# A graph layer on one core: sums kept in PSUM for a block, residual added from PSUM, one buffer for products

## The chip, the cores and the metric

The kernel runs on one core of a Trainium2 chip. The metric is the device time of one execution in microseconds (us). Engines are named as in the profile: PE (TensorE matmuls), PEld (its weight loads), DVE (VectorE), ACT (ScalarE), POOL (GpSimd) and SP (SyncE, which issues most of the transfers). Each engine works through its own queue in order, and semaphores hold an instruction until what it reads is written and what it overwrites is read.

## The reference

There are 6,250 nodes with 64 features and 206,250 edges, sorted by their destination node.

```
h   = relu(layernorm(x))                       # 6250 x 64
msg = h[src] + edge_attr                       # 206250 x 64
agg = segment_sum(msg, dst)                    # 6250 x 64
out = x + relu(agg @ W1 + b1) @ W2 + b2        # 64 -> 128 -> 64
```

## The kernel before

The sum over the edges is split in two. For the features of nodes, `h[src]`, most edges are handled without a gather. A matrix of counts (how often node s feeds node d) is made by matmuls of masks, and then multiplied by h. For the features of edges, matmuls of masks with the edges' own rows give the sums directly.

**Blocks and steps.** The nodes are taken in 23 blocks (`NW`). The first 22 have 14 steps each, and the last has 10. `count(b, s)` at each step makes the counts of six lists of edges. PE runs six products of masks into a PSUM tile `pc` (line 868), and ACT copies the tile to `counts` in SBUF (line 871). There are two `pc` tiles, so the products of step n wait for the copy of step n-2. Every third step DVE makes the masks `hot_lo` and `hot_key` of three steps (line 858), with two buffers each.

**Products.** The counts of block b-1 are multiplied by h during steps 0 to 6 of block b (`multiply`, line 888). They accumulate in a PSUM tile `pv`, of which there are two. At step 3 `chunk_place` (line 461) adds the edges' sums of block b-1 into the same `pv`. At step 10 `add_products` (line 900) lets DVE add `pv` to the sums in SBUF.

**Sums of edges.** A block has up to six chunks of 42 nodes, taken in two at a time. Such a pair is called a set (a unit in the code). At steps 7, 10 and 13 `chunk_sum` runs 24 small matmuls per chunk into one PSUM tile `bank` (line 439). Right behind them ACT copies the set to SBUF as `by_node` (line 442), and SP issues the loads of the set after the next (line 418). `chunk_place` of the next block reads the three copies. In the first block the sums stand at steps 10, 12 and 13, and in the last block at 6 and 8.

**Groups.** The last 20 groups of edges have no counts. POOL gathers rows of h onto their edge features (line 301), and `sum_groups` (line 489) sums two groups at a time, also in `bank`. ACT copies that to `by_group` (line 492). These sums fall on steps 0, 1, 2 or 4 of some blocks.

**Layers.** For a block of nodes whose sum is complete, `mlp` puts five parts on the steps n, n+2, n+9, n+10 and n+11, with n at step 8 or 11. `mlp_hidden` multiplies by W1 (line 936) and ACT applies relu (line 938). `mlp_product` multiplies by W2 into the PSUM tile `po` (line 943), and ACT copies it to `y` (line 949). `bias` adds b2 to the rows of x (line 928). `mlp_add` adds those to `y` on DVE (line 954), and `mlp_store` sends `y` out. At the very end `mlp_out` (line 959) adds from `po` without a copy.

**Order.** The order of each engine's queue is written out by hand. The loop over `steps` at the end of the program emits the work of a step in a fixed order: `before` entries, count, multiply, place, add, layers, then the entries put there by `at(step, ...)`, and last the groups. Where a gather stands is planned with times written into the program (`pool_until`). [...]

The opening, up to about 40 us, normalises x, finds where the lists of edges begin and packs them. There `by_quarters` (line 651) uses `pv` tiles for four small products `psrcq`.

Of the kernel before, what the change touches and what calls it, by code (L numbers as in the profile page):

```python
# [116 lines left out]
AHEAD = 16  # L117
OPENING_US = 15.0
# [3 lines left out]
def gnn_kernel(ctx: ExitStack, tc: tile.TileContext, x, src_t, dst_t, dst_g, edge, w1, b1, w2, b2, out):  # L122
# [277 lines left out]
    bank = ps.tile([P, GB * D], F32, name="bank", bufs=1)  # L400
# [5 lines left out]
    assert sum(n for _, _, n in units) == NC  # L406
    unplaced = [sum(1 for unit in units if unit[0] == b) for b in range(NW)]
# [24 lines left out]
    def chunk_sum(u):  # L432
        n = units[u][2]
        hot, feat = hot_of.pop(u), feats.pop(u)
        for i in range(n):
            for k in range(JP):
                for q in range(JQ):
                    j = q * JP + k
                    nc.tensor.matmul(bank[q * QP:q * QP + WQ, i * D:(i + 1) * D], hot[:, i, j, :], feat[i][:, j, :],  # L439
                                     start=(k == 0), stop=(k == JP - 1))  # L440
        by_node[u] = work.tile([P, GB, D], F32, name="by_node", bufs=3)
        nc.scalar.activation(by_node[u][:, :n].rearrange("p c d -> p (c d)"), bank[:, :n * D], AF.Copy)  # L442
        load(u + 2)

# [9 lines left out]
    def chunk_place(u):  # L454
        b, c, n = units[u]
        of = by_node.pop(u)
# [27 lines left out]
    def sum_groups(g, hot, tiles):  # L484
        for b in range(GB):
            for k in range(PK):
                for q in range(PQ):
                    j = q * PK + k
                    nc.tensor.matmul(bank[q * QP:q * QP + WQ, b * D:(b + 1) * D], hot[:, b, j, :],  # L489
                                     tiles[b][:, j, :], start=(k == 0), stop=(k == PK - 1))  # L490
        by_node["h", g] = work.tile([P, GB, D], F32, name="by_group", bufs=1)
        nc.scalar.activation(by_node["h", g].rearrange("p b d -> p (b d)"), bank, AF.Copy)  # L492
# [152 lines left out]
    def by_quarters(t0, t1):  # L645
        rows = src_s.bitcast(F32)
        for t in range(t0, t1):
            own = slice(t * QP, (t + 1) * QP)
            px = ps.tile([P, 512], F32, tag="pv", name="psrcq")[:, :GP * PK]
# [225 lines left out]
    def open_pv(b):  # L875
        pvs[b] = [ps.tile([P, 512], F32, tag="pv", name="pv")[:, :BN], 0]
# [62 lines left out]

    def mlp_rows(b, tag="po", bufs=1):  # L940
        po = ps.tile([P, 2, D], F32, tag=tag, name="po", bufs=bufs)
# [4 lines left out]
    def mlp_product(b):  # L946
        po = mlp_rows(b)
        y = late.tile([NP, 2, D], F32, name="y", bufs=2)
        nc.scalar.activation(y[:pairs[b]], po[:pairs[b]], AF.Copy)  # L949
        outs[b] = y  # L950

    def mlp_add(b):
        y = outs[b]
        nc.vector.tensor_tensor(y[:pairs[b]], y[:pairs[b]], xs.pop(b)[:pairs[b]], op=OP.add)
# [148 lines left out]
    ADDED, LOADED = 10, 2  # L1103
# [17 lines left out]
    for u, (b, c, _) in enumerate(units):  # L1121
# [4 lines left out]
        at(n, chunk_sum, u)  # L1126

# [211 lines left out]
```

## Time and profile before

| what | value |
|---|---|
| median of 3 runs | 489.25 us (488.44 to 490.86) |
| the profiled execution | 489.07 us, span 487.2 us |
| PE busy | 424.2 us (87%) |
| DVE busy | 415.1 us (85%) |
| POOL busy | 388.3 us (80%) |
| ACT busy | 366.0 us (75%) |

A group's row in the profile reads: line, engine, operation, output <- inputs by the program's names, shapes, count, then busy us, mean ns of one, and the idle time of the engine before them with what ended it. A row of the timeline reads: start in us from the begin of the span, length in us, engine, line, operation, and in brackets the idle time of the engine before it and what ended that. Rows of one kind that follow each other are merged (x12 stands for 12 matmuls). The ends of matmuls are modelled, so a few hundredths of a us between PE and another engine mean little.

### The profile page before, as it was taken

To read this page: it belongs to the slowest core of one execution; us is meant where nothing else is said; L and a number is where in the kernel's file an instruction comes from. 1 tells how busy PE (TensorE), PEld (TensorE's weight loads), DVE (VectorE), ACT (ScalarE), POOL (GpSimd) and SP (SyncE) were. 2 spreads that over 40 slices of the span, in tenths; PEclk is the share of its full clock that TensorE was granted. 3 is DMA by queue.
4 is the path that set the end of the run, shared out by engine and by line. 5 is a ranking of instruction groups with operands and counts; after the bars stand their busy time and mean duration, and the time that the engine had idled before them with its cause. 6 is when DMAs were issued, how large, how long until landed. Compare 5 with 4: busy or idle time off the path is not lost.

```text
span 487.2 us, 17218 instructions
## 1 busy us (share of the span) xinstructions
PE 424.2 (87%) x7301; PEld 374.8 (77%) x7302; DVE 415.1 (85%) x561; ACT 366.0 (75%) x607; POOL 388.3 (80%) x239
## 2 busy tenths in 40 slices
PE   3156798998988999999999999989999999999894
PEld 3055687886886888888988978878888888888783
DVE  7888989879999798988998889888998899998751
ACT  3727889878877788788898789777887787786650
POOL 7787888888888888888888888888888888888000
PEclk9655699999999999999999999999999999999998
DMA  9959367378366585784784784675775775764700
GB/s 237 238 172 300 74 147 193 76 180 192 69 167 155 145 228 122 176 230 105 192 220 98 172 228 94 170 201 125 187 187 124 201 179 122 203 158 93 213 13 16
DMA packets 122378, 77.98 MB, mean 160 GB/s; under 512 B 34768, under 2 KB 120728, under 8 KB 122072
## 3 DMA queue, kind: packets, MB, share of 16 engines
q1 hardware_dynamic: 97464, 66.88, 47.1%
q0 software_dynamic: 24592, 9.19, 15.0%
q8 instruction: 59, 0.97, 0.8%
q10 hardware_dynamic: 240, 0.75, 0.5%
q14 instruction: 23, 0.19, 0.1%
HBM read 72.80 MB, written 3.99 MB: 158 GB/s over the span
## 4 chain that ended last, share of the span: by engine, by line
PE 68%; ACT 13%; DMA 6%; issue 5%; DVE 4%; POOL 3%; DVEq 0%; ACTq 0%; POOLq 0%
PE pv L888 26%; PE pc L868 22%; PE bank L439 11%; ACT counts L871 9%; POOL rows L301 3%; DMA feat<-in_edge 3%; PE po L943 2%; PE pv L461 2%; DMA dstq<-in_dst_g,cols_i 2%; ACT junk L694 1%; PE ph L936 1%; PE bank L489 1%; DVE hot_key L858 1%; DVE hot_lo L858 1%; DMA firsts_i<-in_dst_g 1%
## 5 line engine op out<-in xcount | busy, mean ns | idle before, releaser
L301 POOL DMA_INDIRECT pfeat<-table,src_p x160 | 334.0, 2088 | 49.7 <-issue 43.0
L871 ACT ACTIVATE counts<-pc 128x882 fp32r<-128x882 f32 x318 | 282.1, 916 | 49.1 <-PE pc L868 39.8
L868 PE MATMUL pc<-hot_key,hot_lo 128*128 128x147 bf16 x1908 | 179.2, 232 | 22.9 <-ACT counts L871 13.6
L858 DVE TENSOR_TENSOR hot_lo<-iota_lo,keys 128x2304 bf16<-128x2304 bf16 (+1 forms) x107 | 143.8, 1344 | 36.2 <-PE pc L868 29.0
L888 PE MATMUL pv<-counts,h 128*128 128x252 f32 (+1 forms) x1127 | 171.0, 292 | 0.2
L868 PEld LDWEIGHTS <-hot_lo 128*128 128x128 bf16 x1908 | 130.5, 100 | 45.4 <-issue 24.2
L858 DVE TENSOR_TENSOR hot_key<-iota_key,keys 128x2664 bf16<-128x2664 bf16 (+1 forms) x107 | 163.3, 1526 | 0.0
L888 PEld LDWEIGHTS pv<-counts,h 128*128 128x128 f32 x1127 | 143.5, 190 | 0.6 <-ACT counts L871 0.5
L439 PE MATMUL bank<-feat,hot 128*21 128x64 f32 x3240 | 69.0, 222 | 5.9 <-issue 3.0
L439 PEld LDWEIGHTS bank<-feat,hot 128*21 128x21 f32 x3240 | 52.3, 101 | 18.3 <-issue 6.8
L427 DVE TENSOR_TENSOR hot<-rel,iota 128x504 f32<-128x504 bf16 x68 | 45.6, 671 | 0.1
L442 ACT ACTIVATE by_node<-bank 128x128 f32<-128x128 f32 x68 | 19.0, 280 | 18.4 <-PE bank L439 12.4
L301 POOL DMA_INDIRECT words<-packed,first_i x15 | 20.8, 1385 | 4.6 <-issue 3.4
L301 POOL DMA_INDIRECT rows<-in_dst_g,row_i x15 | 17.4, 1162 | 5.2 <-issue 4.0
L943 PE MATMUL po<-w2s,hid 128*126 128x64 f32 (+2 forms) x100 | 16.8, 288 | 1.7 <-ACT hid L938 1.2
L943 PEld LDWEIGHTS po<-w2s,hid 128*126 128x126 f32 (+2 forms) x100 | 13.5, 192 | 5.7 <-ACT hid L938 1.9
L936 PE MATMUL ph<-sums,w1s 128*128 128x252 f32 (+2 forms) x50 | 16.1, 404 | 0.2 <-ACT y L949 0.2
L900 DVE TENSOR_TENSOR sums<-sums,pv 128x252 f32<-128x252 f32 (+4 forms) x31 | 9.8, 339 | 6.7 <-PE pv L888 5.9
L492 ACT ACTIVATE by_group<-bank 128x128 f32<-128x128 f32 x10 | 2.8, 277 | 15.1 <-PE bank L489 11.1
L938 ACT ACTIVATE hid<-ph,b1s 128x252 f32<-128x252 f32 (+2 forms) x25 | 11.6, 464 | 2.3 <-PE ph L936 2.3
L461 PE MATMUL pv<-select,by_node 128*64 128x42 f32 (+1 forms) x272 | 12.6, 234 | 0.0
L461 PEld LDWEIGHTS pv<-select,by_node 128*64 128x64 f32 x272 | 9.9, 137 | 3.0
(202 smaller groups left out, 252.3 us busy)
## 6 DMA issues: line engine op xcount, KB each, us to landing
feat<-in_edge SPq DMA_DIRECT2D x135, 384.0 KB
pfeat<-in_edge SPq DMA_DIRECT2D x20, 256.0 KB
pfeat<-table,src_p POOLq DMA_INDIRECT x160
xl<-in_x SPq DMA_DIRECT2D x2, 768.0 KB
xs<-in_x SPq DMA_DIRECT2D x23, 63.0 KB
out_y<-y SPq DMA_DIRECT2D x23, 63.0 KB
dstn<-in_dst_g SPq DMA_DIRECT2D x1, 1024.0 KB
table<-xl SPq DMA_DIRECT2D x1, 800.0 KB
```

The costliest lines, as they stand in the source:

```text
L301: nc.gpsimd.indirect_dma_start(out=rows, out_offset=None, in_=source, in_offset=bass.IndirectOffsetOnAxis(ap=index, axis=0), compute_op=op)
L427: nc.vector.tensor_tensor(hot_of[u][:, :n].rearrange("p c j w -> p (c j) w"), rel[:, c:c + n].rearrange("p c q k -> p (c q k)").unsqueeze( ...
L439: nc.tensor.matmul(bank[q * QP:q * QP + WQ, i * D:(i + 1) * D], hot[:, i, j, :], feat[i][:, j, :], start=(k == 0), stop=(k == JP - 1))
L442: nc.scalar.activation(by_node[u][:, :n].rearrange("p c d -> p (c d)"), bank[:, :n * D], AF.Copy)
L461: nc.tensor.matmul(pvs[b][0][i * D:(i + 1) * D, k:k + z - a], of[:, i, :], select[:, a - low:z - low], start=False, stop=False)
L858: nc.vector.tensor_tensor(hot[:, :n].rearrange("p t (m o) -> p t m o", o=2), iota_k.rearrange("p (m o) -> p m o", o=2).unsqueeze(1).to_bro ...
L868: nc.tensor.matmul(pc[:, k, m * K:(m + 1) * K], hot_lo[:, j, :], hot_key[:, j, :K], start=True, stop=True)
L871: nc.scalar.activation(ring[:, (2 * b + half) % 3, :, i * ST * V:(i + 1) * ST * V].rearrange("p h (k m) -> p h k m", k=2), pc[:, :, :ST // ...
L888: nc.tensor.matmul(pv[:, :2 * half].rearrange("p (k n) -> p k n", k=2), h2[:, h, :], of[:, :, h, :half], start=(h == 0), stop=(h == HI - 1))
L936: nc.tensor.matmul(ph[:, :n], w1s, agg[:, start[b]:start[b + 1]], start=True, stop=True)
L938: nc.scalar.activation(outs[b][:, :n], ph[:, :n], AF.Relu, bias=b1s)
L943: nc.tensor.matmul(po[:pairs[b], k, :], outs[b][:, k:2 * pairs[b]:2], w2s, start=True, stop=True)
```

## The change

The PSUM tile `bank` grows from one set to four (a whole 2 KiB bank). Three are for a block's sets and one for groups. `chunk_sum` writes each set to its own place and no longer copies. For a block but the last, one ACT instruction copies all its sets at step 1 of the next block (`chunk_copy`, `COPIED = 1`). In the last block each set is copied alone, right behind its sums, as before. `by_node` becomes one tile for a whole block instead of three for sets.

`mlp_product` writes to one of four places in a PSUM tile of its own, `rows_p`, and ACT no longer copies it. `mlp_add` adds the residual on DVE straight from PSUM into a new `y`.

The bank for `rows_p` comes from `pv`, which has one buffer instead of two.

```diff
+SETS = 3
...
-    bank = ps.tile([P, GB * D], F32, name="bank", bufs=1)
+    bank = ps.tile([P, SETS + 1, GB, D], F32, name="bank", bufs=1)
     nc.vector.memset(bank, 0.0)
...
+    set_of = [sum(1 for v in units[:u] if v[0] == units[u][0]) for u in range(len(units))]
...
     def chunk_sum(u):
...
-                    nc.tensor.matmul(bank[q * QP:q * QP + WQ, i * D:(i + 1) * D], hot[:, i, j, :], feat[i][:, j, :],
+                    nc.tensor.matmul(bank[q * QP:q * QP + WQ, set_of[u], i, :], hot[:, i, j, :], feat[i][:, j, :],
                                      start=(k == 0), stop=(k == JP - 1))
-        by_node[u] = work.tile([P, GB, D], F32, name="by_node", bufs=3)
-        nc.scalar.activation(by_node[u][:, :n].rearrange("p c d -> p (c d)"), bank[:, :n * D], AF.Copy)
         load(u + 2)
+
+    def chunk_copy(b, u0, u1):
+        if b not in by_node:
+            by_node[b] = work.tile([P, SETS, GB, D], F32, name="by_node", bufs=1)
+        k0, k1 = set_of[u0], set_of[u1] + 1
+        nc.scalar.activation(by_node[b][:, k0:k1].rearrange("p k c d -> p (k c d)"),
+                             bank[:, k0:k1].rearrange("p k c d -> p (k c d)"), AF.Copy)
...
     def chunk_place(u):
-        of = by_node.pop(u)
+        of = by_node[b][:, set_of[u]]
...
     def sum_groups(g, hot, tiles):
-                    nc.tensor.matmul(bank[q * QP:q * QP + WQ, b * D:(b + 1) * D], hot[:, b, j, :],
+                    nc.tensor.matmul(bank[q * QP:q * QP + WQ, SETS, b, :], hot[:, b, j, :],
...
-            px = ps.tile([P, 512], F32, tag="pv", name="psrcq")[:, :GP * PK]
+            px = ps.tile([P, 512], F32, tag="pv", name="psrcq", bufs=1)[:, :GP * PK]
...
-        pvs[b] = [ps.tile([P, 512], F32, tag="pv", name="pv")[:, :BN], 0]
+        pvs[b] = [ps.tile([P, 512], F32, tag="pv", name="pv", bufs=1)[:, :BN], 0]
...
+    rows_p = ps.tile([P, 4, 2, D], F32, name="rows_p", bufs=1)
+    turn_p = [0]
+
     def mlp_rows(b, tag="po", bufs=1):
-        po = ps.tile([P, 2, D], F32, tag=tag, name="po", bufs=bufs)
+        if tag == "pr":
+            po = rows_p[:, turn_p[0] % 4]
+            turn_p[0] += 1
+        else:
+            po = ps.tile([P, 2, D], F32, tag=tag, name="po", bufs=bufs)
...
     def mlp_product(b):
-        po = mlp_rows(b)
-        y = late.tile([NP, 2, D], F32, name="y", bufs=2)
-        nc.scalar.activation(y[:pairs[b]], po[:pairs[b]], AF.Copy)
-        outs[b] = y
+        outs[b] = mlp_rows(b, "pr")

     def mlp_add(b):
-        y = outs[b]
-        nc.vector.tensor_tensor(y[:pairs[b]], y[:pairs[b]], xs.pop(b)[:pairs[b]], op=OP.add)
+        po = outs[b]
+        outs[b] = late.tile([NP, 2, D], F32, name="y", bufs=2)
+        nc.vector.tensor_tensor(outs[b][:pairs[b]], po[:pairs[b]], xs.pop(b)[:pairs[b]], op=OP.add)
...
-    ADDED, LOADED = 10, 2
+    ADDED, LOADED, COPIED = 10, 2, 1
...
         at(n - 1, chunk_hot, u)
         at(n, chunk_sum, u)
+        if b == NW - 1:
+            at(n, chunk_copy, b, u, u)
+        elif unplaced[b] == i + 1:
+            at(first_step[b + 1] + COPIED, chunk_copy, b, u - i, u)
```

3 lines of the change are left out of this document (2 added, 1 removed).

## The prediction

> **What bounds the kernel now.** I read the page first, then the busy time of each engine in the steady stretch, the waits of TensorE, ScalarE and VectorE there, the groups of instructions of the lines that the diff touches, and last the timeline of a few blocks. The profiled execution took 489.07 us for a span of 487.2; the median of the runs is 489.25, so the two stand within 0.2 us, and the sum below is made against 489.07.
>
> ```profile
> 60.00:460.00 400.00, 374.09 (x6706) 331.80 (x6695) 357.36 (x446) 321.01 (x520) 340.55 (x168) 1.00 0.66 163
> ```
>
> In this row of the windows view (length, then PE, PEld, DVE, ACT and POOL busy, clock, DMA share), PE is busy 374 of 400 us and ACT 321. The steady stretch can give back at most PE's 26 us of idle time, and only what ends on ACT can answer to this change. The waits in 60 to 470 us:
>
> ```profile
> PE pc L868 <- ACT counts L871: 12.2, 24, 1.0
> PE bank L439 <- issue: 3.0, 9, 0.5
> PE bank L439 <- DMA feat<-in_edge: 2.0, 2, 1.4
> ...
> PE ph L936 <- ACT y L949: 0.2, 1, 0.2
> ```
> ```profile
> ACT counts L871 <- PE pc L868: 38.5, 89, 1.2
> ```
>
> Each row is total us, times, longest. PE waits 12.2 us for ACT to empty a buffer of products (pc), and ACT waits 38.5 us for PE to fill one. PE is the bound with ACT close behind. The change takes copies out of ACT's queue, so the question is how much of the 12.2 us those copies cause.
>
> **The terms.** Groups by line over the span (busy us, mean ns, idle before):
>
> ```profile
> L442 ACT ACTIVATE by_node<-bank 128x128 f32<-128x128 f32 x68 | 19.0, 280 | 18.4 <-PE bank L439 12.4 <-PE pc L868 4.0 <-PE pstart L343 1.0
> L954 DVE TENSOR_TENSOR y<-y,xs 126x128 f32<-126x128 f32 (+1 forms) x23 | 6.6, 289 | 4.1 <-ACT y L949 2.6 <-issue 0.4
> L949 ACT ACTIVATE y<-po 126x128 f32<-126x128 f32 (+1 forms) x23 | 6.3, 275 | 1.6 <-PE po L943 0.7 <-issue 0.7
> L392 ACT ACTIVATE rel<-pdst 128x384 bf16<-128x384 f32 x5 | 2.5, 490 | 2.7 <-issue 1.6 <-PE pdst L391 1.0
> L959 DVE TENSOR_TENSOR y<-po,xs 126x128 f32<-126x128 f32 (+1 forms) x2 | 0.6, 290 | 2.0 <-PE po L943 2.0
> ```
>
> Of the 68 copies by_node, 66 (three a block in 22 blocks) become 22 copies of 384 columns, and the last block keeps its two. A copy of 384 columns out of PSUM is in the trace: 490 ns. The 23 copies y go away. A block with one layer has ACT work of 3 x 280 + 275 = 1,115 ns less in its steps 7 to 13 and 490 ns more in step 1. Over the run that is 66 x 0.280 + 23 x 0.275 - 22 x 0.490 = 14.0 us less ACT work. If every us of it held up PE the time would be 475; what counts is what PE waits for.
>
> **Copies after the sums.** Block 2, where PE is at steps 11 to 13:
>
> ```profile
> 97.06 0.28 ACT L442 ACTIVATE by_node<-bank 128x128 f32<-128x128 f32 x1 [0.72 <-PE bank L439]
> 97.44 1.71 ACT L871 ACTIVATE counts<-pc 128x882 fp32r<-128x882 f32 x2
> ```
> ```profile
> 96.84 0.96 PE L868 MATMUL pc<-hot_key,hot_lo 128*128 128x147 bf16 x12
> 98.40 0.49 PE L868 MATMUL pc<-hot_key,hot_lo 128*128 128x147 bf16 x5 [0.61 <-ACT counts L871]
> ```
>
> PE starts step 11's six products at 96.84. Six take 0.56 us (a row at 255.29 below), so they end at 97.40. The copy ends at 97.34, before that, and counts starts at 97.44, when its products are there. Step 13 has to wait for that counts whether the copy is in the queue or not: two steps of bare products (1.0 us) stand against products plus counts (1.5 us). This 0.61 us wait is in the trace 14 times, first and last here:
>
> ```profile
> 94.79 0.55 PE L868 MATMUL pc<-hot_key,hot_lo 128*128 128x147 bf16 x6 [0.61 <-ACT counts L871]
> ...
> 453.19 0.55 PE L868 MATMUL pc<-hot_key,hot_lo 128*128 128x147 bf16 x6 [0.61 <-ACT counts L871]
> ```
>
> That is 14 x 0.61 = 8.5 us of ACT waits that I leave standing. Seven shorter ones lie at step 10, behind the copy of step 7:
>
> ```profile
> 227.37 0.55 PE L868 MATMUL pc<-hot_key,hot_lo 128*128 128x147 bf16 x6 [0.24 <-ACT counts L871]
> ...
> 449.78 0.55 PE L868 MATMUL pc<-hot_key,hot_lo 128*128 128x147 bf16 x6 [0.30 <-ACT counts L871]
> ```
>
> One of the seven, block 18:
>
> ```profile
> 391.49 0.91 ACT L871 ACTIVATE counts<-pc 128x882 fp32r<-128x882 f32 x1 [0.47 <-PE pc L868]
> 393.30 0.28 ACT L442 ACTIVATE by_node<-bank 128x128 f32<-128x128 f32 x1 [0.90 <-PE bank L439]
> 393.47 0.91 ACT L871 ACTIVATE counts<-pc 128x882 fp32r<-128x882 f32 x1
> ```
> ```profile
> 392.50 0.82 PE L868 MATMUL pc<-hot_key,hot_lo 128*128 128x147 bf16 x6
> ...
> 394.43 0.29 PE L868 MATMUL pc<-hot_key,hot_lo 128*128 128x147 bf16 x2 [0.26 <-ACT counts L871]
> ```
>
> The products end at 393.32, and counts starts at 393.47. Where no copy is in the way it starts 0.05 after them (255.85 to 255.90 below), so the copy costs 0.10 us. Seven times that is **-0.7 us**; if all seven waits went, 7 x 0.27 = -1.9. The wait of ph for a copy y, 0.22 us once, goes: **-0.2**.
>
> **The new copy at step 1.** Steps 0 to 3 of block 11:
>
> ```profile
> 252.49 1.75 ACT L871 ACTIVATE counts<-pc 128x882 fp32r<-128x882 f32 x2
> 254.61 0.92 ACT L871 ACTIVATE counts<-pc 128x882 fp32r<-128x882 f32 x1 [0.36 <-issue]
> 255.90 0.92 ACT L871 ACTIVATE counts<-pc 128x882 fp32r<-128x882 f32 x1 [0.37 <-PE pc L868]
> ```
> ```profile
> 255.29 0.56 PE L868 MATMUL pc<-hot_key,hot_lo 128*128 128x147 bf16 x6
> 255.66 1.08 PE L888 MATMUL pv<-counts,h 128*128 128x252 f32 x7
> 256.67 0.43 PE L461 MATMUL pv<-select,by_node 128*64 128x42 f32 x8
> ```
>
> The copy takes 254.24 to 254.73, mostly inside ACT's idle 0.36 us; the 0.12 that is left is gone in the next 0.37. chunk_place, which now waits for this copy on its own, starts at 256.67: 1.9 us to spare. The tightest case that I found is block 2, where ACT also clears sums. There the counts of steps 1 to 3 come back to back:
>
> ```profile
> 84.52 2.51 ACT L871 ACTIVATE counts<-pc 128x882 fp32r<-128x882 f32 x3
> ```
> ```profile
> 86.84 0.55 PE L461 MATMUL pv<-select,by_node 128*64 128x42 f32 x12
> ```
>
> Step 1's ends near 85.4, the copy near 85.9, place 0.9 later. So I take nothing from block 2 on. That cover is ACT's idle time while PE multiplies; without it the copy costs 0.49 us a block. Block 1 has no cover: ACT is behind from its start, and PE waits for it at step 9.
>
> ```profile
> 75.67 0.55 PE L868 MATMUL pc<-hot_key,hot_lo 128*128 128x147 bf16 x6 [1.02 <-ACT counts L871]
> ```
>
> The new copy lies ahead of this wait, and the copy that step 7 loses lies behind it but ahead of step 10. So the cost is between 0 and 0.5 us; I take **+0.3**.
>
> **The residual from PSUM.** L959 already adds from PSUM: 290 ns against 289 for L954 from SBUF. I take nothing. [...]
>
> **One buffer for pv.** It is freed by the add at step 10 and taken again at step 0 of the next block. VectorE runs ahead there: in block 18 the add starts at 392.02, before PE begins step 8's products at 392.50, and the buffer is taken again six steps later:
>
> ```profile
> 392.02 0.40 DVE L900 TENSOR_TENSOR sums<-sums,pv 128x252 f32<-128x252 f32 x1
> ```
>
> In the opening two of the four psrcq tiles now follow each other in one buffer, so the second waits for a small copy by ACT; the nearest row, a by_node copy, bounds that by +0.3. PE's next products wait for VectorE's masks there, so I take zero.
>
> The memset of bank grows to 512 columns. Such a memset takes 0.48 us elsewhere in the opening:
>
> ```profile
> 3.99 0.48 DVE L265 MEMSET spread<- 128x512 f32 x1 [0.17 <-issue]
> ```
>
> VectorE has idle time for ScalarE soon after it, before the words are packed:
>
> ```profile
> 14.91 1.22 DVE L598 SCALAR_TENSOR_TENSOR dstn<-dstn,srcl 96x1024 int32<-96x1024 int32 x1 [0.27 <-ACT srcl L595]
> ```
>
> So I take zero here too, and at most +0.5.
>
> DMA issues, SP's queue (loads and stores in the same order, store still after the add) and POOL's are moved past nothing. If PE does gain, the late one next is the load of the third set, which already ended two waits of 2.0 us together.
>
> **Sum:** 489.07 - 0.7 - 0.2 + 0.3 = **488.5 us**. Less than 0.5% (2.4 us) is about what a measurement of this kernel cannot tell from no change. With every bounded term at its low end the sum is 489.07 - 1.9 - 0.2 = 487.0, with every one at its high end 489.07 + 0.5 + 0.3 + 0.5 = 490.4.
>
> **Rivals.** *Faster: ACT is the bound of steps 7 to 13, and its relief spreads.* For it: the copies sit among ACT's busiest rows, and 12.2 us of PE waits end on ACT. Against it: the rows at 97.06, where the copy ends before its successor could start. If all 12.2 goes, 476.9; if half, 483. The third set's loads would stop it before the full gain. 0.20.
>
> *Slower: the copy at step 1 is late.* It stands in front of counts of step 2, which frees the buffer for step 4, and place waits for it. If it is wholly uncovered, 22 x 0.49 = +10.8, so 499.3; it decides from 0.11 us a block (2.4 us). For it: block 1, and extra ACT work in early steps. Against it: 0.9 us to spare in the tightest block. 0.15.
>
> *Slower by sharing banks.* Sums of sets and of groups, and four layers' rows, now share one bank each. [...] As a mechanism of this kernel: each of the 10 group sums of PE waits for a copy of 490 ns and one counts of 916 ns before it, 10 x 1.4 = 14 us at most, 502; hidden for those at step 0 and 4. Before, group sums and set sums already share a tile, and all PE waits for ACT other than those for counts come to little in the view above. 0.03.
>
> No change: 0.62, its own range 487.0 to 490.4. The range reaches to the half case of the faster rival and to a third of the slower one (488.5 + 3.6): **483 to 492**. Beyond it I leave 0.05 below and 0.14 above. By the cases: faster 0.20, same 0.62, slower 0.18.
>
> **What would show it.** Right: 24 copies by_node, 22 of them near 490 ns, PE's wait for counts still above 9 us, with the 0.61 us waits still there; adds from PSUM near 290 ns; no new releaser of more than 1 us on PE. Wrong on the fast side: those 0.61 us waits shrink. Wrong on the slow side: place (pv from by_node) waiting for ACT, multiply waiting for VectorE's add, or longer waits of PE for counts in steps 3 to 6.

## The result

The kernel after takes 492.63 us (median of 16 runs), the kernel before in the same comparison 489.64 (16 runs). The ratio is 1.0066 (95% interval 1.0039 to 1.0093): slower by 0.66%, some 3.2 us. The forecast was 488.5 us with a range up to 492 us and "no change" as the likeliest case, and both are wrong. Executions that came out more than 1.5% above the fastest of their kernel are left out of the ratios here and below, and the traces of bank_only and step13_memset, taken in such executions (497.05 and 504.77 us), are read only up to block 1.

The profiled execution of after took 492.71 us, span 490.8, against 489.07 and 487.2 before. The rows of after that answer to those of the prediction are these. First the page's busy times, then the steady stretch from 60 to 460 us (length, then PE, PEld, DVE, ACT and POOL busy, clock, DMA share, GB/s):

```profile
PE 424.8 (87%) x7301; PEld 375.6 (77%) x7302; DVE 415.7 (85%) x561; ACT 353.7 (72%) x540; POOL 387.2 (79%) x239
```
```profile
60.00:460.00 400.00, 371.68 (x6670) 329.21 (x6664) 354.87 (x446) 307.05 (x453) 338.68 (x168) 1.00 0.65 161
```

ACT did lose its work: 366.0 us became 353.7. But PE is busy 371.7 of these 400 us in place of 374.1, so it waits more. The waits in 60 to 470 us (total us, times, longest):

```profile
PE pc L877 <- ACT counts L880: 13.1, 27, 0.7
...
PE pdst L392 <- ACT sum_p L521: 1.1, 1, 1.1
...
PE bank L497 <- ACT by_node L450: 0.5, 1, 0.5
```
```profile
ACT counts L880 <- PE pc L877: 65.2, 110, 1.9
```

PE's waits for counts grew from 12.2 to 13.1 us although ACT has less to do, and ACT now waits 65.2 us for PE in place of 38.5. The groups of the moved operations came out as forecast:

```profile
L450 ACT ACTIVATE by_node<-bank 128x384 f32<-128x384 f32 x22 | 10.6, 483 | 0.0
```
```profile
L968 DVE TENSOR_TENSOR y<-rows_p,xs 126x128 f32<-126x128 f32 (+1 forms) x23 | 6.6, 288 | 3.8 <-PE rows_p L959 2.9 <-PE pc L877 0.5
```

So the loss is not in the price of an operation. To find its place I took the length of each block, from the start of its first product (six `pc<-hot_key,hot_lo` in a row) to that of the next block, out of TensorE's timeline. It is one execution of each kernel, and each lies within 0.6 us of its kernel's median:

| stretch | before, us | after, us | difference |
|---|---|---|---|
| up to block 1 | 61.98 | 62.70 | +0.72 |
| block 1 | 19.72 | 19.94 | +0.21 |
| blocks 2 to 21 | 373.73 | 376.42 | +2.69 |
| block 22 and the end | 31.78 | 31.74 | -0.04 |

Sixteen of the twenty blocks from 2 to 21 differ by 0.35 us at most, mostly downward. Four are longer: block 8 by 0.76, block 10 by 0.85, block 11 by 0.61 and block 17 by 1.14 us. The four together lost 3.4 us. The experiments ask what happened there, and in the opening.

### The profile page after: what moved, and what is told of

Same layout as the page of the kernel before. It is cut to its first block, busy times and chain, and to the rows that moved or that the text cites. A ratio compares the mean times of both kernels' runs of the same rounds, so it can differ in the third digit from the quotient of the medians.

```text
span 490.8 us, 17112 instructions
## 1 busy us (share of the span) xinstructions
PE 424.8 (87%) x7301; PEld 375.6 (77%) x7302; DVE 415.7 (85%) x561; ACT 353.7 (72%) x540; POOL 387.2 (79%) x239
## 4 chain that ended last, share of the span: by engine, by line
PE 68%; ACT 17%; issue 5%; DVE 4%; DMA 4%; SPq 1%; DVEq 0%; ACTq 0%
PE pv L897 24%; PE pc L877 23%; ACT counts L880 12%; PE bank L441 10%; PE pv L469 2%; DMA feat<-in_edge 2%; PE rows_p L959 2%; ACT junk L703 1%; PE psrcq L660 1%; PE bank L497 1%; DMA firsts_i<-in_dst_g 1%; PE ph L945 1%; ACT inrow L318 1%; DVE hot_lo L867 1%; DVE hot_key L867 1%
## 5 line engine op out<-in xcount | busy, mean ns | idle before, releaser
L867 DVE TENSOR_TENSOR hot_lo<-iota_lo,keys 128x2304 bf16<-128x2304 bf16 (+1 forms) x107 | 143.9, 1345 | 39.7 <-PE pc L877 32.7
L959 PE MATMUL rows_p<-w2s,hid 128*126 128x64 f32 (+1 forms) x92 | 15.6, 290 | 0.8 <-issue 0.6
L959 PEld LDWEIGHTS rows_p<-w2s,hid 128*126 128x126 f32 (+1 forms) x92 | 12.4, 192 | 3.3 <-issue 0.9
L450 ACT ACTIVATE by_node<-bank 128x384 f32<-128x384 f32 (+1 forms) x24 | 11.2, 466 | 0.0
```

The source lines that it names most:

```text
L450: nc.scalar.activation(by_node[b][:, k0:k1].rearrange("p k c d -> p (k c d)"), bank[:, k0:k1].rearrange("p k c d -> p (k c d)"), AF.Copy)
L867: nc.vector.tensor_tensor(hot[:, :n].rearrange("p t (m o) -> p t m o", o=2), iota_k.rearrange("p (m o) -> p m o", o=2).unsqueeze(1).to_bro ...
L959: nc.tensor.matmul(po[:pairs[b], k, :], outs[b][:, k:2 * pairs[b]:2], w2s, start=True, stop=True)
```

## The experiments

The theories, as the expectations name them: A, the waits come from ScalarE's one copy at step 1, where ScalarE has other early work; B, the loss comes from the opening, through the psrcq tiles, or from the one buffer for pv; C, half each. Their failure led to D (where TensorE's code is cut), E (where GpSimd's gathers of words fall) and F (the fill of `bank` displaces those gathers from the start).

Each kernel was timed beside the kernel before on one chip. Different groups of runs, each with its own time of before, were on different chips, so ratios of different groups compare only within their intervals. A trace is of one execution. In the edits below "..." stands for lines that are left out.

### Which part, and which place

*One part alone: residual_only.*

```diff
-    bank = ps.tile([P, SETS + 1, GB, D], F32, name="bank", bufs=1)
+    bank = ps.tile([P, GB * D], F32, name="bank", bufs=1)
...
+        by_node[u] = work.tile([P, GB, D], F32, name="by_node", bufs=3)
+        nc.scalar.activation(by_node[u][:, :n].rearrange("p c d -> p (c d)"), bank[:, :n * D], AF.Copy)
         load(u + 2)
...
```

> The change without its first part: three copies of 128 columns a block behind their sums as before; residual from PSUM and one buffer pv as after. Theory A (the whole loss of 0.66% comes from the one copy of 384 columns at step 1, in the blocks where ScalarE has other early work): 0.998 to 1.000 of the kernel before, 488.7 to 489.7 us. Theory B (the loss comes from the opening, where the psrcq tiles now share one buffer, or from one buffer for pv): 1.005 to 1.007, 492 to 493 us. Theory C (half each): 1.003.

*The other part alone: bank_only.*

```diff
...
-        outs[b] = mlp_rows(b, "pr")
+        po = mlp_rows(b)
+        y = late.tile([NP, 2, D], F32, name="y", bufs=2)
+        nc.scalar.activation(y[:pairs[b]], po[:pairs[b]], AF.Copy)
+        outs[b] = y
...
```

> The first part alone: the one copy of 384 columns at step 1 of the next block; residual through ScalarE's copy y and two buffers pv as before. Theory A: 1.005 to 1.008 of the kernel before, 492 to 493.5 us (a little more than after, since the copies y stay). Theory B: 0.998 to 1.000. Theory C: 1.003.

*The small products of the opening kept apart: psrcq_apart.*

```diff
...
-            px = ps.tile([P, 512], F32, tag="pv", name="psrcq", bufs=1)[:, :GP * PK]
+            px = rows_p[:, t].rearrange("p k d -> p (k d)")[:, :GP * PK]
```

> The kernel after with the four psrcq tiles in four parts of the bank that rows_p takes, so that none waits for the copy of the one before. Theory A: as after, 1.0066 of the kernel before. Theory B, if the opening is its place: 0.999 to 1.001 and the opening 0.7 us or more shorter (first product at 37.5 us in place of 39.7); if pv's one buffer is its place, as after.

*The one copy at step 13 of its own block: copy_step13.*

```diff
-    ADDED, LOADED, COPIED = 10, 2, 1
+    ADDED, LOADED, COPIED = 10, 2, -1
```

> The kernel after with the one copy of 384 columns behind the third set's sums, at step 13 of its own block, in place of step 1 of the next. Theory A, with the loss in what stands behind the copy at steps 1 to 9: the loss goes, 0.998 to 1.000, since the copy now stands where the third copy of 128 columns stood and is 0.21 us longer. Theory B: as after, 1.005 to 1.007. If any copy of 490 ns between two counts costs PE its excess: 22 x 0.21 = 4.6 us, 1.009.

Measured against before (489.76 us): residual_only 1.0056 (1.0017 to 1.0095), bank_only 1.0085 (1.0041 to 1.0129), psrcq_apart 1.0111 (1.0060 to 1.0162), copy_step13 1.0018 (0.9989 to 1.0048).

Each part alone is slower by about as much as both together, though costs of two separate steps would add up. Theory A does not fit residual_only (0.998 to 1.000 expected), theory B does not fit bank_only (the same range) and lies just above the interval of copy_step13 (1.005 to 1.007), and theory C's 1.003 lies outside the interval of bank_only. So none of them fits all four. But copy_step13 comes nearest to before, and A's range for it overlaps its interval, so a part of the loss may hang on the place of the copy. In the traces block 8 is 0.85 us longer in residual_only, which has only the second part of the change, and 1.14 us longer in copy_step13. Blocks 10 and 17 are within 0.12 us of before in both, and long (0.84 and 1.12 us) in psrcq_apart. psrcq_apart brings TensorE's first product from 39.7 to 38.2 us, and yet block 1 starts at 63.67 us, so the psrcq tiles do not set the start.

### Code, the shared bank, and the price of the copy

*TensorE's code shifted by 128 instructions: after_shift and before_shift.*

```diff
             a, z = max(-(-i * P // CV), c0), min(-(-(i + 1) * P // CV), c1)
+            if c0 == 0 and i == 6:
+                pad = ps.tile([P, 16], F32, tag="po", name="pad", bufs=1)
+                for _ in range(64):
+                    nc.tensor.matmul(pad, identb, identb[:, :16], start=True, stop=True)
```

> The kernel after with 64 more small products on TensorE in an idle stretch of the opening (their result is used by nobody), so that all of its code behind them lies 128 instructions further on. Theory D (the 0.76 us that block 8 lost against before and the 0.61 us of block 11 hang on where TensorE's code is cut, since its rows show gaps put down to issue and late signals there): blocks 8 and 11 change by more than 0.3 us each, and so do others; the ratio to before moves away from 1.0066, to between 1.002 and 1.009. Theory A (the losses are waits for ScalarE's work and keep their places): blocks 8, 10, 11 and 17 are again 0.76, 0.85, 0.61 and 1.14 us longer than before within 0.1, and the ratio is 1.006 to 1.008.

> The kernel before with the same 64 small products. Theory D: single blocks change by more than 0.3 us against before, in either direction, and the ratio lies between 0.997 and 1.005. Theory A: no block from 2 on changes by more than 0.2 us, and the ratio is 0.999 to 1.002.

*The sums of groups in another bank: group_apart. It fills 384 columns of bank and 128 of rows_p.*

```diff
...
-                    nc.tensor.matmul(bank[q * QP:q * QP + WQ, SETS, b, :], hot[:, b, j, :],
+                    nc.tensor.matmul(rows_p[q * QP:q * QP + WQ, 3, b, :], hot[:, b, j, :],
...
-            po = rows_p[:, turn_p[0] % 4]
+            po = rows_p[:, turn_p[0] % 3]
...
```

> The kernel after with the sums of groups in the bank of rows_p (three turns there in place of four), so that they share no bank with the copy of 384 columns. If the shared bank costs what its one wait shows: block 10 gets 0.5 us back, all others stay, and the ratio is 1.005 to 1.006. If the shared bank is the cause of block 17's late copy by_group too: blocks 10 and 17 get 1.5 us back, ratio 1.003 to 1.004. If neither: as after, 1.0066.

*The copy made twice: copy_twice.*

```diff
+        for _ in range(2 if b < NW - 1 else 1):
-        nc.scalar.activation(by_node[b][:, k0:k1].rearrange("p k c d -> p (k c d)"),
+            nc.scalar.activation(by_node[b][:, k0:k1].rearrange("p k c d -> p (k c d)"),
```

> The kernel after with the copy of 384 columns made twice at step 1, so 0.49 us more of ScalarE's work a block. Theory A (the copy is covered by idle time in most blocks and costs where ScalarE has other early work): most blocks keep their length within 0.1 us, and blocks with such work (8, 10, 11, 17) lose up to 0.5 us each more, so 493.5 to 495, ratio 1.008 to 1.012. If the copy is uncovered everywhere: +10.8 us, ratio 1.028. If it is covered everywhere and the losses are of another kind: as after, 1.0066.

Measured against before (488.55 us): after_shift 1.0139 (1.0102 to 1.0176), before_shift 1.0327 (1.0280 to 1.0374), group_apart 1.0119 (1.0074 to 1.0164), copy_twice 1.0127 (1.0088 to 1.0167). In both shifted kernels the added products delayed the opening (block 1 at 66.83 and 65.11 us), so only their blocks are compared.

In after_shift blocks 8, 10, 11 and 17 are 0.73, 0.86, 0.58 and 0.74 us longer than before, as in after but for block 17 (1.14 there). So theory D falls: the losses stay at their places in the program when the code moves. But before_shift was not what theory A expected either: its blocks 5 and 6 are 2.42 and 2.26 us longer, with the steady code untouched.

copy_twice adds 0.48 us of ScalarE's work to each block and its blocks 2 to 21 take 377.76 us in place of 376.42: 1.34 us for some 10 us of work. Block 1 is 0.55 us longer than in after. So a second copy is nearly covered from block 2 on, and not covered in block 1. The median, 494.79 us, lies in theory A's range of 493.5 to 495, but that tells little: group_apart, with one copy, has about the same ratio. group_apart removes one wait, and its trace shows it. First TensorE at steps 1 and 2 of block 10 in after, then in group_apart:

```profile
235.58 1.07 PE L897 MATMUL pv<-counts,h 128*128 128x252 f32 x7
237.16 0.65 PE L497 MATMUL bank<-pfeat,hotp 128*21 128x64 f32 x32 [0.51 <-ACT by_node L450]
```
```profile
235.54 1.07 PE L899 MATMUL pv<-counts,h 128*128 128x252 f32 x7
236.54 0.65 PE L499 MATMUL rows_p<-pfeat,hotp 128*21 128x64 f32 x32
```

The wait of 0.51 us is gone, but block 10 is still 0.62 us longer than before, where it was 0.85. So only some 0.2 us of its loss go with the shared bank, and group_apart's own ratio is no better than after's.

### GpSimd's gathers

In block 8 the trace shows something odd. ScalarE is idle for 1.98 us although the six products that it waits for were issued by 208.51. TensorE, then ScalarE of after:

```profile
207.57 0.30 PE L877 MATMUL pc<-hot_key,hot_lo 128*128 128x147 bf16 x2
208.09 0.42 PE L877 MATMUL pc<-hot_key,hot_lo 128*128 128x147 bf16 x4 [0.21 <-issue]
208.35 0.63 PE L945 MATMUL ph<-sums,w1s 128*128 128x252 f32 x2
```
```profile
206.24 0.92 ACT L880 ACTIVATE counts<-pc 128x882 fp32r<-128x882 f32 x1 [0.49 <-PE pc L877]
209.13 0.91 ACT L880 ACTIVATE counts<-pc 128x882 fp32r<-128x882 f32 x1 [1.98 <-PE ph L945]
```

By the modelled ends the signal came 0.6 us late. The profile does not tell whether the products ended later than modelled or their signal was late. Before, the same copy waits 0.22 us. What stands just ahead of this place is a pair of gathers of words on GpSimd (128 rows of 128 words each; the expectations below call them 4 KB rows, which is wrong). The pair came later into block 8 than it did before. GpSimd of after (block 8 starts at 194.63), then of before (193.95):

```profile
203.96 1.87 POOL L302 DMA_INDIRECT words<-packed,first_i  x1 [0.30 <-issue]
206.13 0.97 POOL L302 DMA_INDIRECT words<-packed,first_i  x1 [0.30 <-issue]
```
```profile
202.30 1.52 POOL L301 DMA_INDIRECT words<-packed,first_i  x1 [0.30 <-issue]
204.12 1.13 POOL L301 DMA_INDIRECT words<-packed,first_i  x1 [0.30 <-issue]
```

That is 9.33 us into block 8 in after, and 8.35 before. In block 11 the pair came 2.0 us earlier than before, and in block 17 the last gather of words came ahead of the block's start in place of 4.34 us into it. So theory E: the losses hang on where these gathers fall. Two pairs of runs test it.

*Without these gathers: before_nowords and after_nowords.*

```diff
...
     def fetch_pair(i0):
         n = min(2, IC - i0)
+        if i0 > 4:
+            words_of[i0] = last_words[0]
+            return
...
```

> The kernel before without GpSimd's gathers of words behind the third pair (the third pair's words are unpacked again in their place, so the sums are not the reference's). Theory E (in the runs so far TensorE's signals of finished products reach ScalarE up to 2.4 us late just behind these gathers of 4 KB rows, and the gaps of TensorE put down to issue lie there): some of TensorE's issue gaps go (5.5 us in blocks 1 to 21 now), and the blocks 5, 8, 11, 14, 17 and 20 get 0.2 to 0.6 us shorter each, 1 to 3 us in all. If the gathers do no harm: every block as before within 0.1 us.

> The kernel after, with the same gathers left out (its sums are not the reference's). Theory E: blocks 8, 11 and 17 lose no more than 0.2 us each against the same blocks of the kernel before without these gathers; what is left of the 2.7 us of steady loss is block 10's 0.85 at most, so blocks 2 to 21 together are between 1.0 us shorter and 0.3 us longer than there. Theory A (waits for ScalarE's copy): blocks 10, 11 and 17 lose 0.8, 0.6 and 1.1 us as before, and the pair differs by 2.7 us.

*The gathers elsewhere in GpSimd's order: before_ahead20 and after_ahead20.*

```diff
-AHEAD = 16
+AHEAD = 20
```

> The kernel before with the gathers of words put into GpSimd's order 20 steps ahead of their use in place of 16, so one or two gathers sooner. Theory E: single blocks (8, 11, 14, 17, 20, or the ones ahead of them) change by 0.3 to 1.2 us; the sum over blocks 2 to 21 moves by 0.5 to 3 us in either direction. Theory A: no block changes by more than 0.2 us.

> The kernel after with the same 20 steps. Theory E: the losses of blocks 8, 11 and 17 move to other blocks or go; block 10's stays. Theory A: 0.76, 0.85, 0.61 and 1.14 us in blocks 8, 10, 11 and 17 again.

With words that are not its own, the program goes on to work off all edges one group after another, so the whole time of the first pair (4,467 and 4,455 us) is not read, only blocks 2 to 21. They take 373.31 us in before_nowords and 373.64 in after_nowords. The difference is 0.33 us where it was 2.69 (0.03 above the bound that theory E gave), and blocks 8, 11 and 17 differ by 0.05, 0.03 and 0.02 us. Without the gathers hardly anything is left of the steady loss, as theory E said and theory A did not. Other blocks of the pair still differ by up to 0.5 us in either direction, and these differences cancel. For before_nowords theory E missed: of the six blocks that it named four are 0.3 to 0.6 us shorter and two 0.3 us longer, and blocks 2 to 21 are only 0.42 us shorter in place of 1 to 3. The issue gaps of TensorE stayed too (4.9 us between 80 and 455 us, 5.3 before), so that half of theory E is wrong.

The second pair shows how much the place of these gathers matters. before_ahead20 is at 1.0138 (1.0106 to 1.0170) and after_ahead20 at 1.0172 (1.0121 to 1.0223); blocks 2 to 21 take 381.32 and 381.86 us, 7.6 us more than in before where theory E allowed 0.5 to 3, but nearly the same in both. Block 8 alone is 4.91 us longer in before_ahead20. There the pair comes right at the sums of groups. TensorE, ScalarE and GpSimd of before_ahead20:

```profile
194.83 0.65 PE L489 MATMUL bank<-pfeat,hotp 128*21 128x64 f32 x32
```
```profile
199.46 0.28 ACT L492 ACTIVATE by_group<-bank 128x128 f32<-128x128 f32 x1 [3.71 <-remote]
```
```profile
195.21 1.10 POOL L301 DMA_INDIRECT words<-packed,first_i  x1 [0.30 <-issue]
196.61 0.97 POOL L301 DMA_INDIRECT words<-packed,first_i  x1 [0.30 <-issue]
```

The sums were issued by 195.48 and ScalarE's copy of them starts at 199.46, 4 us later. "Remote" says that the profile does not tell what ended that wait.

Four more runs moved or split the pairs.

*GpSimd held up ahead of one pair by seven or twenty small fills: before_delay1 and before_delay3.*

```diff
...
+        for _ in range(7 if i0 // 2 in (4,) else 0):     # 20 in before_delay3
+            nc.gpsimd.memset(idle, 0.0)
```

> The kernel before with seven small fills (about 0.15 us each, 1 us together) on GpSimd ahead of one pair of gathers of words, the pair that falls into block 8. Theory E (the place of the pair against TensorE's steps decides): the pair starts at 9.3 us into block 8 in place of 8.35, as it does in after, and block 8 gets 0.5 to 1.0 us longer; all blocks ahead of it keep their length. Theory A: no block changes by more than 0.2 us.

> The same with twenty fills, about 3 us. Theory E: block 8 changes by another amount than with 1 us, anything from -0.3 to +1.0 us, and later blocks (11, 14, 17) may change by 0.3 us or more, since GpSimd's order stays displaced. Theory A: no block changes by more than 0.2 us.

*The two gathers of a pair kept apart: after_split and before_split.*

```diff
...
+            gather(words_of[i0][:, 0, :], packed[:, :], first_i[:, i0:i0 + 1])
+            queue.insert(2, (WORDS_US / 2, lambda to=words_of[i0]: gather(
+                to[:, 1, :], packed[:, :], first_i[:, i0 + 1:i0 + 2])))
...
```

> The kernel after with the two gathers of each pair of words kept apart by two gathers of groups' features. If two gathers of 4 KB rows in a row do the harm: blocks 8 and 11 lose no more than 0.2 us against before, the steady stretch is 1.3 us or more shorter than in after, ratio to before 0.999 to 1.004. If one such gather does it: losses of 0.3 to 1 us each in other blocks, 1.005 to 1.012.

> The kernel before with the same split. If two in a row do the harm: 0.996 to 1.000 of the kernel before. If one does it: single blocks gain or lose 0.3 to 1 us, 0.998 to 1.008.

The ratios, against before at 491.47 us: before_delay1 0.9996 (0.9961 to 1.0030), before_delay3 1.0048 (0.9997 to 1.0099), after_split 1.0019 (0.9991 to 1.0046), before_split 0.9973 (0.9940 to 1.0007). The delay of 1 us missed its aim: the pair came at 7.66 us into block 8, not at 9.3, because GpSimd had come out of the opening otherwise than in the profiled execution of before, and block 8 kept its length (+0.06 us). So the direct test failed to set the place. Block 6, ahead of the fills, was 0.76 us longer all the same, against both theories: what differs there is the execution, and not the program. The runs of before_delay3 lie between 486.74 us (the profiled execution) and 500.03 us, and what differs between them was not traced. The split runs came out in the ranges expected of "two in a row do the harm", but their traces do not bear it out. Blocks 2 to 21 of after_split took 378.31 us in the profiled execution, longer than in after, and its block 8 lost 0.41 us where 0.2 was allowed. That execution took 497.34 us, the longest of its 13. The claim is open.

The place of a pair can also be compared across the kernels, with the last group below taken in. This table has all traces read here in which both gathers of the pair lie in the block, but the split ones:

| block | first gather of the pair, us into the block | kernels | block longer than before, us |
|---|---|---|---|
| 8 | 6.3 to 8.4 | before, before_delay1, before_memset3, before_shift | -0.23 to +0.06 |
| 8 | 9.1 to 9.3 | after, residual_only, copy_step13, psrcq_apart, after_shift, group_apart, copy_twice | 0.73 to 1.14 |
| 8 | 0.9 to 1.6 | after_ahead20, before_ahead20 | 1.57 and 4.91 |
| 11 | 4.7 | before, residual_only, before_delay1 | -0.15 to +0.02 |
| 11 | 6.2 | copy_step13 | 0.37 |
| 11 | 2.7 | after, psrcq_apart, after_shift, group_apart, copy_twice, before_memset3, before_shift | 0.55 to 0.75 |

In block 11 the loss goes with the place of the pair and not with the change: before_memset3 and before_shift do not have the change and lose as much. In block 8 all seven kernels with the late pair have the second part of the change. But after_nowords has it too and, without the pair, loses nothing there. Block 17 is less clear. It is 0.09 and 0.11 us longer in residual_only and copy_step13, where its gather lies as in before, but also 0.41 in before_delay1, where it does too, and 0.42 to 1.14 where the gather lies elsewhere.

### Where GpSimd's displacement starts

GpSimd was already late in the opening. Its third and fourth gathers of rows (the first two take 1.17 and 0.96 us everywhere), and VectorE beside them, in the kernel before:

```profile
9.74 0.17 DVE L401 MEMSET bank<- 128x128 f32 x1
...
11.75 1.76 DVE L550 TENSOR_TENSOR xl<-xl,stat 128x1536 f32<-128x1536 f32 x1
13.43 1.22 DVE L598 SCALAR_TENSOR_TENSOR dstn<-dstn,srcl 96x1024 int32<-96x1024 int32 x1
```
```profile
12.54 1.79 POOL L301 DMA_INDIRECT rows<-in_dst_g,row_i  x1 [0.30 <-issue]
14.64 0.95 POOL L301 DMA_INDIRECT rows<-in_dst_g,row_i  x1 [0.30 <-issue]
...
23.07 0.94 POOL L301 DMA_INDIRECT words<-packed,first_i  x1 [0.31 <-issue]
```

The same in after:

```profile
9.68 0.48 DVE L402 MEMSET bank<- 128x512 f32 x1
...
12.12 1.76 DVE L559 TENSOR_TENSOR xl<-xl,stat 128x1536 f32<-128x1536 f32 x1
13.80 2.35 DVE L607 SCALAR_TENSOR_TENSOR dstn<-dstn,srcl 96x1024 int32<-96x1024 int32 x2
```
```profile
12.39 2.30 POOL L302 DMA_INDIRECT rows<-in_dst_g,row_i  x1 [0.30 <-issue]
15.01 1.96 POOL L302 DMA_INDIRECT rows<-in_dst_g,row_i  x1 [0.31 <-issue]
...
24.18 0.95 POOL L302 DMA_INDIRECT words<-packed,first_i  x1 [0.30 <-issue]
```

The third gather ends at 14.33 before, 0.82 us after VectorE's `xl` operation (11.75 + 1.76 = 13.51), and at 14.69 in after, 0.81 us after the same operation (13.88). The fourth gather of before starts at 14.64, when the first `dstn` operation ends (14.65) and VectorE then idles 0.27 us up to 14.91; it takes its normal 0.95 us. In after VectorE is later by the longer fill, the two `dstn` operations run without a gap to 16.15, and the fourth gather ends 0.82 us after that, at 16.97. So the three gathers here that started while VectorE was in one of these operations took 1.79, 2.30 and 1.96 us and ended 0.81 to 0.82 us behind it. By what means VectorE holds a gather up no trace shows. The gathers of rows of h show such holds through the whole kernel. In before 124 of the 160 take more than 1.6 us, and 121 of these end 1.38 to 1.46 us behind a VectorE operation that ran within 0.2 us of their start; the other 36 take 1.54 to 1.60.

The fill of `bank` that became four times as wide thus costs GpSimd 1.1 us: the first gather of words starts at 24.18 in place of 23.07. This holds in all 20 traces. With the fill at its old place and 128 columns wide, or moved away, that gather starts between 22.87 and 23.18 us (nine kernels). With a longer fill it starts between 24.13 and 24.48 (eleven kernels). Two runs changed the fill alone, or moved it.

*The fill longer, and nothing else of the change: before_memset3.*

```diff
...
-    nc.vector.memset(bank, 0.0)
+    for _ in range(3):
+        nc.vector.memset(bank, 0.0)
```

> The kernel before with its fill of bank (128 columns, 0.165 us) made three times, so that VectorE's next operations start about 0.3 us later, as in after; nothing else is changed. Theory F (the later operations of VectorE then hold up two gathers of rows in place of one): the fourth and fifth gathers of rows take about 2.0 and 1.0 us or the third 2.3, all later gathers come 1 to 1.4 us later, block 1 starts at 63.0 to 64.0 us in place of 60.9 to 62.9, and the ratio is 1.002 to 1.005. If the fill does not matter: block 1 at 61.3 to 62.9, ratio 0.998 to 1.002.

*The fill in an idle stretch, with the copy at step 13: step13_memset.*

```diff
-    nc.vector.memset(bank, 0.0)
...
     nc.vector.tensor_copy(firstp.rearrange("o g q -> o (g q)"), firstp_i)
+    nc.vector.memset(bank, 0.0)
...
-    ADDED, LOADED, COPIED = 10, 2, 1
+    ADDED, LOADED, COPIED = 10, 2, -1
```

> The kernel after with the one copy at step 13 of its own block and the fill of bank moved behind the first operation that VectorE makes before it waits for x (an idle stretch of 1.0 us at 16.2 us). Theory F: gathers of rows as in before, block 1 starts at 61.0 to 62.5 us, 1 to 1.5 us sooner than with the fill in its old place, and the ratio is 0.997 to 1.000. If the fill does not matter: block 1 at 63 us or later, ratio 1.0018 as copy_step13.

before_memset3 took 493.28 us against 491.82: 1.0037 (1.0014 to 1.0061). VectorE and GpSimd there:

```profile
9.88 0.70 DVE L402 MEMSET bank<- 128x128 f32 x3
...
12.43 1.76 DVE L551 TENSOR_TENSOR xl<-xl,stat 128x1536 f32<-128x1536 f32 x1
14.11 2.35 DVE L599 SCALAR_TENSOR_TENSOR dstn<-dstn,srcl 96x1024 int32<-96x1024 int32 x2
```
```profile
12.67 2.34 POOL L301 DMA_INDIRECT rows<-in_dst_g,row_i  x1 [0.30 <-issue]
15.31 1.96 POOL L301 DMA_INDIRECT rows<-in_dst_g,row_i  x1 [0.30 <-issue]
...
24.48 0.94 POOL L301 DMA_INDIRECT words<-packed,first_i  x1 [0.30 <-DMA rows<-in_dst_g,row_i]
```

Both gathers are held as in after, and block 1 starts at 63.68 us, as expected. Blocks 2 to 21 take 376.39 us, 2.66 more than in the profiled execution of before, with blocks 6, 11 and 17 longer by 0.79, 0.75 and 0.47 us (before_delay1 has the first of these too, so it may be the execution's). Nothing in that stretch differs from before in its code. So two fills more, of 0.165 us each on VectorE, make the kernel before lose 0.37%, some 1.8 us.

step13_memset has the early gathers of before again (1.78 and 0.94 us, words at 22.93), so moving the fill undoes the displacement there. Block 1 starts at 62.69, and a later gather of rows takes 2.35 us in its trace (2.02 before), so theory F's 61.0 to 62.5 us was missed. Its ratio, 1.0019 (0.9985 to 1.0052), is that of copy_step13, which has the fill in its old place. So the price of the longer fill is shown where it is added to the kernel before, and no gain is shown where it is taken out of a kernel with the change. No version here is shown to beat the kernel before; before_split, at 0.9973, has an interval that reaches past 1.

**A second displacement, ahead of block 8.** residual_only has the narrow fill, and its pair in block 8 comes late all the same. The traces show why. TensorE, VectorE and GpSimd of before at the end of block 7:

```profile
191.38 0.62 PE L936 MATMUL ph<-sums,w1s 128*128 128x210 f32 x2 [0.22 <-ACT y L949]
```
```profile
192.43 1.36 DVE L858 TENSOR_TENSOR hot_lo<-iota_lo,keys 128x2304 bf16<-128x2304 bf16 x1 [0.74 <-PE ph L936]
193.70 1.54 DVE L858 TENSOR_TENSOR hot_key<-iota_key,keys 128x2664 bf16<-128x2664 bf16 x1
```
```profile
193.41 1.79 POOL L301 DMA_INDIRECT pfeat<-table,src_p  x1 [0.30 <-issue]
```

The same in after, where ScalarE makes no copy y and TensorE does not wait for it:

```profile
191.74 0.56 PE L945 MATMUL ph<-sums,w1s 128*128 128x210 f32 x2
```
```profile
192.73 1.36 DVE L867 TENSOR_TENSOR hot_lo<-iota_lo,keys 128x2304 bf16<-128x2304 bf16 x1 [0.29 <-issue]
194.01 1.54 DVE L867 TENSOR_TENSOR hot_key<-iota_key,keys 128x2664 bf16<-128x2664 bf16 x1
```
```profile
194.17 2.80 POOL L302 DMA_INDIRECT pfeat<-table,src_p  x1 [0.30 <-issue]
```

GpSimd's gather is 0.76 us later than before, as the whole block is by then, but TensorE's `ph` only 0.36 and VectorE's masks 0.30. So the gather no longer finds VectorE in `hot_lo` but in the longer `hot_key`. It ends 1.42 us behind `hot_lo` before (195.20) and 1.42 us behind `hot_key` in after (196.97), and the pair behind it comes 1.0 us later into block 8. The seven kernels of the table with the late pair all have this long gather (2.77 to 2.82 us), residual_only among them; the four with the pair at 6.3 to 8.4 us have it at 1.77 to 1.81 us. So block 8's loss comes with the second part of the change, and not with the fill.

## Why the prediction was wrong

**The step that failed** is the one that leaves GpSimd out: DMA issues, SP's queue and POOL's "are moved past nothing". With it the fill of `bank` was priced by VectorE alone: "So I take zero here too, and at most +0.5". Its argument was that VectorE has idle time (0.27 us) soon after the fill. VectorE did absorb it: the packing ends at 16.15 us in after, and at 16.13 before. But that gap was the moment in which a gather of GpSimd got through. Filling it up held GpSimd for 1.1 us, and GpSimd was not in the sum at all. What that costs in the kernel before is shown by before_memset3: +1.8 us (0.7 to 3.0), where the change costs 3.2. The same step made the wait for a copy y a gain of 0.2 us: it did go, but it shifted VectorE's masks against a gather, and block 8 became 0.76 us longer.

How it reaches the end: the first `dstq` gather stands behind the late ones, and in VectorE's queue the masks of block 0's later steps stand behind the work on it. Block 1 starts 17.4 to 18.4 us after the begin of that work in all 20 traces, but the work starts 7.6 to 10.7 us after the gather, so the 1.1 us arrive only in the mean. In the profiled execution of before that work starts at 44.20 us and block 1 at 61.98; in after they are at 44.66 and 62.70, in before_memset3 at 46.03 and 63.68. Over the seven kernels with the narrow fill at its old place block 1 starts at 61.96 us in the mean (60.86 to 63.34), over the ten with a longer one at 63.51 (62.56 to 64.87); the two shifted kernels are left out. That is 1.55 us, of which the profiled execution of after shows only 0.72. In the steady stretch the displaced gathers of words fall to other steps, and blocks 8 and 11 are longer where they do (the table); with these gathers out, 0.33 of 2.69 us is left.

**Copies after the sums: right.** The 0.61 us waits stayed: 16 waits between 0.59 and 0.64 us in after, 17 before (the forecast's 14 leave out three that the profile puts down to something else than `counts`). The seven short waits at step 10 add up to 1.0 us in after and 1.8 before, so 0.8 us shorter against 0.7 forecast. Of their blocks only 13 and 14 got shorter by more than 0.02 us.

**The new copy at step 1: right as to its price, open as to its place.** copy_twice puts 0.07 us a block on a second copy. Block 1, the uncovered one, lost 0.21 us (forecast +0.3) and only 0.02 with the copy at step 13. Block 10 waits 0.51 us once for the bank that the copy shares with the sums of groups, and taking that wait out gave back 0.2 us. This is the rival "slower by sharing banks", in one place instead of ten. I gave that rival 14 us and a chance of 0.03; the mechanism is real, the size is not. The ratio of copy_step13 (1.0018, against 1.0066) leaves open that the copy's place costs more than its length.

**The residual from PSUM: right,** 288 ns against 289. **One buffer for pv: right** as to the end: the psrcq tiles did wait, 1.65 us once where I had bounded it by 0.3, but psrcq_apart, which frees them, starts block 1 no sooner. The cover was not the masks, as I said, but the `dstq` gather.

**The rivals.** "Faster" has nothing for it. "Slower" was given 0.18 in all, on mechanisms of ScalarE and of PSUM. The slower case that came was on an engine pair that the prediction did not look at. The profile of before had it in sight: gathers of 1.79, 1.70 and 2.02 us in the opening among others of 0.95.

**What stays open.** The parts do not add up to the 3.2 us. The fill costs 1.8 us in the kernel before, but the kernel with the fill moved is no faster than copy_step13; 0.8 us of block 8 and 0.2 us each of block 10 and block 1 are seen in traces, and single executions differ by more than that. Whether the copy at step 1 costs something in blocks 10 and 17, which keep their length in residual_only and copy_step13, was not separated from the place of the gathers. Why TensorE's products are seen late behind a gather of words was not found.

## What to carry to other kernels

Where GpSimd issues gathers, read its rows beside VectorE's: here a fill that was 0.31 us longer (0.48 in place of 0.17) made GpSimd 1.1 us late, and the 0.27 us in which VectorE was idle were the slot in which a gather got through. A setup instruction is priced by what it pushes, on every queue whose rows are seen to move with it, not by its own length. Where one part alone and the other part alone each cost as much as both together, look for something that both displace, and not for two prices.

## What was not expected of the hardware

- A held gather of GpSimd ended 0.81 to 0.82 us after the VectorE operation that held it (five held gathers of rows in the rows above), and a free one took 0.95 us. A held gather of rows of h ended 1.38 to 1.46 us after it (121 of them in before), and a free one took 1.54.
- By the modelled ends, TensorE's work was seen by ScalarE 0.6 us late in block 8 of after, 1.4 us behind the end of two gathers of words, and about 4 us late in block 8 of before_ahead20, during two of them.
- After that last wait TensorE's granted clock was 0.50 for 6.8 us (second row, columns as above). In the profiled execution of before the clock was 0.50 too from 40 to 57 us, and six products of masks took 0.90 to 0.92 us there (rows at 42.89, 50.58 and 56.08), but 0.56 at 57.43. So a part of that block's 4.91 us comes from the clock:

```profile
193.60:199.20 5.60, 4.97 (x72) 4.12 (x70) 2.96 (x6) 1.49 (x4) 4.69 (x4) 1.00 1.08 295
200.20:207.00 6.80, 6.10 (x41) 5.72 (x40) 4.75 (x8) 4.64 (x12) 5.89 (x4) 0.50 0.42 84
207.00:213.00 6.00, 5.82 (x98) 5.00 (x98) 5.12 (x7) 3.85 (x5) 5.39 (x3) 1.00 0.23 22
```
